# Reordering three pieces of work around the score row of a two-layer graph kernel

## The chip, the cores and the metric

The kernel runs on one core of one Trainium2 chip. The metric is the device time of one execution in microseconds (us). The traces are of single profiled executions. TensorE, VectorE, ScalarE, GpSimd and SyncE stand in profile lines as PE, DVE, ACT, POOL and SP (SPq is SyncE's own queue, from which it starts transfers).

## The reference, cut to what matters

Sixty-four graphs of 256 nodes with 512 features each pass two layers. Everything is float32.

```python
# layer 0
agg = einsum('bij,bjf->bif', adj, x) / max(sum(adj), 1e-6)
x1  = layernorm(x + relu(concat([x, agg]) @ W.T))
# layer 1
q, k = split(x1 @ Wqk); v = x1 @ Wv
agg  = adj @ (k * mask)
w    = mask * sum(q * agg, -1) / sqrt(512)
out  = layernorm(x1 + softmax(w)[:, :, None] * v)
```

## The kernel before: the parts that the change and the argument touch

The kernel works on 32 pairs of graphs in a software pipeline. One turn of the loop `j` runs layer 0 of pair `j`, layer 1 of pair `j-1`, and the softmax and last norm of pair `j-2`. Each large product is done as seven half-size products (P1 to P7), so VectorE and GpSimd prepare sums of blocks (`x1T_s`, `x1T_i`, `xT_s`, `xT_i`, `tv`, `sa`) and VectorE and ScalarE add up results. The order of instructions on each engine is chosen when the program is built; `tc.issue_after(ins)` and `tc.keep_in_program_order` constrain that choice. `late_work` is a queue of small pieces that the program text deals out between the products.

The products of a pair need the first norm's result `x1` with features on partitions (`x1T`). VectorE transposes 32 x 32 blocks within `own` (128x512 in 0.69 us, mean of 124 in before), and SyncE then places 16 squares, each by one transfer of 64 KB (2.3 us from issue to landing, median). The same SyncE queue carries the scores: a column `d` to DRAM and back as `row`, spread over all partitions, for the softmax.

```python
def place():                                  # in before
    for a in range(P // Q):
        for b in range(P // Q):
            send(to[b*Q:(b+1)*Q, :, a], sq[a*Q:(a+1)*Q, b]...)     # one square of x1T
        if a == 0 and j > 0:
            fetch_scores(j - 1)               # row <- d; d went ahead of place()
    load_x(j + 1); ...

def softmax(j):
    vector[0] = nc.vector.reduce_max(top, rk, ...).ins      # waits for the row
    ...                                       # two pairs of exponentials on ScalarE
    nc.vector.tensor_tensor(p, p, total, op=OP.mult)
```

After the softmax VectorE has the additions of `v` (last norm), and additions that free TensorE's banks: `y<-bank,y` (`after_p7`, L556 in before, L558 in the changed kernel) and `own<-bank,own` (`after_p2` of layer 0, L547). ScalarE copies other banks and also scales the norms' results.

```python
norm0(j); mask_adj(j); sumsM[j] = adj_sums(j)      # before: ahead of layer 1's products
...
run("k h h n k h h a n b q q d n c e q q n g f p p", ...)
```

## Time and profile before

| | before |
|---|---|
| median, us (2 runs) | 2135.93 (2132.95 to 2138.91) |
| span of the profiled run, us | 2142.4 |
| mean granted TensorE clock | 0.967 |
| TensorE's recurring waits, us in all | 139.2 |
| time at half clock, us in all | 95.6 |

"Recurring waits" adds the rows of TensorE's waits that occur four times or more. "Half clock" adds the stretches that the trace grants 0.50, between 110 and 2000 us; a stretch is taken to cost half its length at most. The page line is this one (busy us, share of the span, instructions):

```profile
PE 1960.3 (92%) x6596; PEld 1259.8 (59%) x6596; DVE 1618.3 (76%) x2950; ACT 1063.4 (50%) x2565; POOL 836.0 (39%) x898
```

TensorE is busy 92%, so the whole question is about the remaining 8% and the clock.

### The profile page before, as it was taken

The page shows a single profiled execution, that of the slowest core. Times are in us where ns is not written, and L with a number is a line of the kernel's source. Part 1 is how long each engine was busy: PE and PEld are TensorE (multiplying, and loading weights), DVE is VectorE, ACT ScalarE, POOL GpSimd, SP SyncE. Part 2 cuts the span into 40 slices and gives each one's busy share as a digit, 9 for nine tenths or more (in the row PEclk, how much of TensorE's full clock was granted, in tenths as well). Part 3 has the DMA queues.
Part 4 walks back from the last instruction along what each step waited for, and adds up shares of the span by engine and source line. Part 5 has one row for each costly group of instructions (what it writes and reads, how often), then busy time and mean ns, then how long its engine had stood idle before and what let it go on. Part 6 is the DMA issues. An engine that isn't in the chain of part 4 may idle for free.

```text
span 2142.4 us, 22354 instructions
## 1 busy us (share of the span) xinstructions
PE 1960.3 (92%) x6596; PEld 1259.8 (59%) x6596; DVE 1618.3 (76%) x2950; ACT 1063.4 (50%) x2565; POOL 836.0 (39%) x898
## 2 busy tenths in 40 slices
PE   8699999999999999999999999999999989999996
PEld 4465566566565565665665665655665655665663
DVE  6568777778777778777778777788778787777785
ACT  2354555455555455554455454555454555554553
POOL 2444432444433444424444423444324444334411
PEclk9899999999999999999999999999999999999998
DMA  4322333222343323333223342223332223332211
GB/s 168 74 58 82 93 104 103 66 69 85 94 104 86 83 63 90 94 104 84 70 71 88 103 104 75 65 80 92 104 104 69 69 82 93 104 94 74 64 51 45
DMA packets 389114, 182.16 MB, mean 85 GB/s; under 512 B 272128, under 2 KB 353664, under 8 KB 388992
## 3 DMA queue, kind: packets, MB, share of 16 engines
q1 hardware_dynamic: 388992, 180.72, 31.3%
q8 instruction: 53, 0.87, 0.2%
q14 instruction: 69, 0.57, 0.1%
HBM read 114.10 MB, written 34.06 MB: 69 GB/s over the span
## 4 chain that ended last, share of the span: by engine, by line
PE 47%; DVE 32%; ACT 9%; issue 5%; DMA 4%; POOL 2%; SPq 1%; DVEq 0%; ACTq 0%; POOLq 0%
PE bank L134 47%; DVE own L426 4%; DVE v L499 4%; DVE own L427 4%; DMA out<-v 3%; DVE st L404 3%; ACT own L414 2%; ACT v L414 2%; DVE y L586 2%; DVE tv L344 2%; DVE y L556 2%; DVE own L547 2%; ACT row L487 1%; POOL x1T_i L255 1%; DVE tv L343 1%
## 5 line engine op out<-in xcount | busy, mean ns | idle before, releaser
L134 PE MATMUL bank<-w,x1T_s 128*128 128x512 f32 x512 | 283.7, 663 | 0.0
L134 PE MATMUL bank<-tv,sa 128*128 128x256 f32 x768 | 197.6, 387 | 38.0 <-ACT agg L377 38.0
L134 PE MATMUL bank<-w,xT_s 128*128 128x512 f32 x512 | 231.1, 593 | 0.0
L255 POOL TENSOR_TENSOR x1T_i<-x1T 128x256 f32<-128x256 f32 x32 | 26.8, 838 | 521.1 <-DMA x1T<-turn 480.6
L134 PEld LDWEIGHTS bank<-tv,sa 128*128 128x128 f32 x768 | 143.4, 191 | 85.3 <-ACT agg L377 50.4
L297 ACT COPY bank<-bank 128x256 f32<-128x256 f32 x192 | 68.7, 358 | 214.2 <-PE bank L134 214.2
L263 POOL TENSOR_TENSOR sa<-adj 128x256 f32<-128x256 f32 x64 | 61.5, 962 | 280.1 <-DMA adj<-adj_t 147.8
L426 DVE SCALAR_TENSOR_TENSOR own<-z,rdeg,own 128x512 f32<-128x512 f32 x128 | 165.4, 1312 | 1.1 <-ACT z L395 1.1
L319 DVE TENSOR_TENSOR bank<-bank,fifth 128x256 f32<-128x256 f32 x256 | 102.7, 427 | 76.6 <-ACT fifth L310 73.6
L134 PE MATMUL bank<-t,xT_s 128*128 128x512 f32 (+1 forms) x384 | 159.0, 523 | 0.0
L134 PE MATMUL bank<-t,x1T_s 128*128 128x512 f32 (+1 forms) x384 | 158.5, 521 | 0.0
L409 ACT ACTIVATE rstd<-mv,eps 128x2 f32<-128x2 f32 x128 | 37.9, 296 | 237.1 <-DVE mv L405 234.8
L414 ACT ACTIVATE v<-v,shift,rstd 128x512 f32<-128x512 f32 x128 | 97.2, 806 | 114.5 <-DVE shift L412 114.5
L134 PEld LDWEIGHTS bank<-w,xT_s 128*128 128x128 f32 x512 | 96.6, 190 | 96.7 <-issue 80.6
L427 DVE SCALAR_TENSOR_TENSOR own<-own,x 128x512 f32<-128x512 f32 x128 | 148.2, 1195 | 0.0
L134 PE MATMUL bank<-t_i,x1T_i 128*128 128x256 f32 x384 | 118.0, 389 | 31.8 <-POOL x1T_i L255 31.8
L134 PEld LDWEIGHTS bank<-w,x1T_s 128*128 128x128 f32 x512 | 110.1, 215 | 59.5 <-issue 47.6
L134 PE MATMUL bank<-own,adj 128*128 128x256 f32 x256 | 80.2, 442 | 69.4 <-DVE y L586 69.4
L307 ACT COPY bank<-bank 128x512 f32<-128x512 f32 x192 | 111.3, 580 | 55.3 <-PE bank L134 55.3
L134 PE MATMUL bank<-t_i,xT_i 128*128 128x256 f32 x384 | 117.1, 388 | 23.0 <-POOL xT_i L255 14.4
L134 PEld LDWEIGHTS bank<-t_i,xT_i 128*128 128x128 f32 x384 | 74.0, 194 | 102.3 <-issue 70.2
L414 ACT ACTIVATE own<-own,shift,rstd 128x512 f32<-128x512 f32 x128 | 103.9, 813 | 44.7 <-DVE shift L412 44.7
(171 smaller groups left out, 4708.7 us busy)
## 6 DMA issues: line engine op xcount, KB each, us to landing
xT<-x_t SPq DMA_DIRECT2D x64, 512.0 KB, 4.9
x<-x SPq DMA_DIRECT2D x64, 512.0 KB, 4.7
out<-v SPq DMA_DIRECT2D x64, 512.0 KB, 2.8
x1T<-turn SPq DMA_DIRECT2D x496, 64.0 KB, 2.3
adj<-adj_t SPq DMA_DIRECT2D x64, 256.0 KB, 2.9
turn<-adj SPq DMA_DIRECT2D x64, 256.0 KB, 4.8
row<-d SPq DMA_DIRECT2D x31, 256.0 KB, 5.2
wqk<-wqk_t SPq DMA_DIRECT2D x4, 512.0 KB, 5.3
```

The lines of the kernel that those rows point to most:

```text
L134: i = nc.tensor.matmul(ps, a, b, start=start, stop=True, skip_group_check=True)
L255: eng.tensor_add(i[0], a21, a22)
L263: nc.gpsimd.tensor_add(s[:, 0], a21, a22)
L297: nc.scalar.copy(q[0][:, :HF], lo)
L307: nc.scalar.copy(q[1].rearrange("p (h f) -> p h f", h=2), lo[:, None, :].to_broadcast([P, 2, HF]))
L319: nc.vector.tensor_add(q[k][:, HF:], q[k][:, HF:], fifth[0])
L344: nc.vector.tensor_sub(t2, b22, t1)
L404: nc.vector.bn_stats(st, src[:, t])
L414: nc.scalar.activation(src[:, t], src[:, t], AF.Identity, bias=shift[:, t:t + 1], scale=rstd[:, t:t + 1])
L426: nc.vector.scalar_tensor_tensor(o, z[:, k, t], rdeg[:, k, t:t + 1], o, op0=OP.mult, op1=OP.add)
L427: nc.vector.scalar_tensor_tensor(o, o, 0.0, xs[j][:, k, t], op0=OP.max, op1=OP.add)
L499: nc.vector.scalar_tensor_tensor(v[k][:, t], v[k][:, t], probs[j][:, k, t:t + 1], x1[:, k, t], op0=OP.mult, op1=OP.add)
```

## The change

Its intent, as far as the diff shows: cure the three waits that lead TensorE's list in before. The first layer norm goes behind the additions of P2 onto `q` (L587), so that they free the bank in time; GpSimd's sums of the masked adjacency move one turn later, and its inner sums keep their program order; and eight of the 16 squares go ahead of the scores, so that `x1T` is complete earlier. The additions to `own` and `y` are tied behind the softmax. The order of TensorE's products after P2 changes a little too (`q q d n c e q q` becomes `q d q n c q e q`).

```diff
-            eng.tensor_add(i[0], a21, a22)            # and three more inner sums
+            for to, op, c, d in (...):
+                tc.keep_in_program_order(eng.tensor_tensor(to, c, d, op=op))
...
 def after_p2(fifth):                                  # layer 0
+    with behind(tops[0]):                             # behind the softmax's last product
         nc.vector.tensor_add(own[:, k, 0], o[k], own[:, k, 0])
 def after_p7(k):
+    with behind(tops[1]):
         nc.scalar.copy(yt[:, k, 1], u[k])
+    with behind(tops[0]):
         vector[0] = nc.vector.tensor_add(yt[:, k, 1], y[k], yt[:, k, 1]).ins
...
             run("i f k f", i=i, k=k, f=open1)
+            places[0](range(2))                       # eight squares
             send_scores(j - 2)
+            places[0]((2,))                           # four
+            fetch_scores(j - 2)
+            places[0]((3,))                           # four
...
+            sumsM[j - 1] = adj_sums(j - 1)            # a period later
-        norm0(j)
         mask_adj(j)
-        sumsM[j] = adj_sums(j)
...
-            run("k h h n k h h a n b q q d n c e q q n g f p p", ...)
+            run("k h h n k", k=k, h=h, n=n)
+            norm0(j, vector[0])                       # behind the P2 addition onto q
+            run("h h a n b q d q n c q e q n g f p p", ...)
```

More of the change, by code (lines that the diff above doesn't have):

```diff
@@ L28 @@
 from collections import deque
-from contextlib import ExitStack
+from contextlib import ExitStack, nullcontext
 import concourse.bass as bass
@@ L129, in run, with behind @@
             units[name].pop(0)()
-    vector = [None]
+    vector, places, tops = [None], [None], [None, None]
+    def behind(ins):
+        return tc.issue_after(ins) if ins else nullcontext()
     def mm(ps, a, b, start=False):
@@ L254, in inner_sums @@
             i = [X.i[:, r, ks] for r in range(4)]
-            eng.tensor_add(i[0], a21, a22)
-            eng.tensor_sub(i[1], i[0], a11)
-            eng.tensor_sub(i[2], a11, a21)
-            eng.tensor_sub(i[3], a12, i[1])
+            for to, op, c, d in ((i[0], OP.add, a21, a22), (i[1], OP.subtract, i[0], a11),
+                                 (i[2], OP.subtract, a11, a21), (i[3], OP.subtract, a12, i[1])):
+                tc.keep_in_program_order(eng.tensor_tensor(to, c, d, op=op))
     def adj_sums(j):
@@ L318, in last_two @@
                 for k in range(2):
-                    nc.vector.tensor_add(q[k][:, HF:], q[k][:, HF:], fifth[0])
+                    vector[0] = nc.vector.tensor_add(q[k][:, HF:], q[k][:, HF:], fifth[0]).ins
                 soon(0.8)
@@ L416, in layer_norm, with norm0 @@
         return [(0.8, lambda t=t: stats(t)) for t in range(n)], [(0.2, scale)]
-    def norm0(j):
+    def norm0(j, after=None):
         own, z, rdeg = owns[j], zs.pop(j), rdegs.pop(j)
@@ L425, in combine @@
             o = own[:, k, t]
-            nc.vector.scalar_tensor_tensor(o, z[:, k, t], rdeg[:, k, t:t + 1], o, op0=OP.mult, op1=OP.add)
+            with behind(after):
+                nc.vector.scalar_tensor_tensor(o, z[:, k, t], rdeg[:, k, t:t + 1], o, op0=OP.mult, op1=OP.add)
             nc.vector.scalar_tensor_tensor(o, o, 0.0, xs[j][:, k, t], op0=OP.max, op1=OP.add)
@@ L446, in turn, with place @@
             nc.vector.transpose(sq[:, :, k, :, t].rearrange("p b c q -> p c b q"), owns[j][:, k, t])
-        def place():
-            for a in range(P // Q):
+        def place(r):
+            for a in r:
                 for b in range(P // Q):
@@ L452, in place @@
                          sq[a * Q:(a + 1) * Q, b].rearrange("p k c t q -> p (k c t) q"))
-                if a == 0 and j > 0:
-                    fetch_scores(j - 1)
-            load_x(j + 1)
-            if j + 2 < NP:
-                load_rows(j + 2)
-        return [(0.7, lambda k=k, t=t: turn(k, t)) for k in range(2) for t in range(NT)] + [(0.0, place)]
+        places[0] = place
+        return [(0.7, lambda k=k, t=t: turn(k, t)) for k in range(2) for t in range(NT)]
     def scale_scores(j, to):
@@ L482, in softmax @@
         rk = row.rearrange("p a (k c) -> p k a c", k=2)
-        vector[0] = nc.vector.reduce_max(top, rk, axis=AX.XY, negate=True).ins
+        nc.vector.reduce_max(top, rk, axis=AX.XY, negate=True)
         total = small.tile([P, 2], F32, name="total")
@@ L488, in softmax @@
                                  accum_out=total[:, k:k + 1])
-            nc.scalar.activation(p[:, k], w[:, k * NT:(k + 1) * NT], AF.Exp, bias=top[:, k:k + 1])
+            tops[1] = nc.scalar.activation(p[:, k], w[:, k * NT:(k + 1) * NT], AF.Exp, bias=top[:, k:k + 1]).ins
         nc.vector.reciprocal(total, total)
-        nc.vector.tensor_tensor(p, p, total[:, :, None].to_broadcast([P, 2, NT]), op=OP.mult)
+        tops[0] = nc.vector.tensor_tensor(p, p, total[:, :, None].to_broadcast([P, 2, NT]), op=OP.mult).ins
     def finish(j):
@@ L546, in after_p2 @@
             for k in range(2):
-                nc.vector.tensor_add(own[:, k, 0], o[k], own[:, k, 0])
+                with behind(tops[0]):
+                    nc.vector.tensor_add(own[:, k, 0], o[k], own[:, k, 0])
             add_fifth(own[:, :, 0, HF:], fifth)
@@ L554, in after_p7 @@
         def after_p7(k):
-            nc.scalar.copy(yt[:, k, 1], u[k])
-            add = nc.vector.tensor_add(yt[:, k, 1], y[k], yt[:, k, 1])
-            vector[0] = add.ins
+            with behind(tops[1]):
+                nc.scalar.copy(yt[:, k, 1], u[k])
+            with behind(tops[0]):
+                vector[0] = nc.vector.tensor_add(yt[:, k, 1], y[k], yt[:, k, 1]).ins
             soon()
@@ L585, in after_p2 @@
             for k in range(2):
-                nc.vector.tensor_add(q[:, k], o[k], q[:, k])
+                vector[0] = nc.vector.tensor_add(q[:, k], o[k], q[:, k]).ins
             add_fifth(q[:, :, HF:], fifth)
@@ L652, in resnorm_kernel @@
             run("i k i k i k i k", i=i, k=k)
+            places[0](range(4))
         else:
             run("i f k f", i=i, k=k, f=open1)
+            places[0](range(2))
             send_scores(j - 2)
+            places[0]((2,))
+            fetch_scores(j - 2)
+            places[0]((3,))
             run("i f k f i f k i f k", i=i, k=k, f=open1)
-        flush()
+        if j > 0:
+            sumsM[j - 1] = adj_sums(j - 1)
+            load_x(j)
+            if j + 1 < NP:
+                load_rows(j + 1)
         run("m p p m p p", m=m, p=p)
@@ L704, in resnorm_kernel @@
             open1 = pairs(u2, Y, A22, W1["T4"], b4) + pairs(y2, Y, S4, W1["B22"], b3)
-            run("k h h n k h h a n b q q d n c e q q n g f p p", k=k, h=h, n=n, q=q, p=open1, **g)
+            run("k h h n k", k=k, h=h, n=n)
+            norm0(j, vector[0])
+            run("h h a n b q d q n c q e q n g f p p", h=h, n=n, q=q, p=open1, **g)
+            flush()
             b8()
             py, pu = pu, py
+        else:
+            norm0(0)
+            flush()
     j = NP - 1
@@ L715, in resnorm_kernel @@
     flush()
+    sumsM[j] = adj_sums(j)
     T = sums_T(owns[j])
```

## The prediction

> **What bounds the kernel now.** I read the page, then TensorE's waits, then the timeline of one steady period, then SyncE's own rows in it. The loop runs 32 times; the score maximum (L483) recurs every 64.9 us, so about 30 such periods make the span. The waits, in total, times and longest:
>
> ```profile
> PE bank L134 <- DVE y L586: 69.4, 30, 2.8
> PE bank L134 <- ACT agg L377: 38.0, 31, 2.1
> PE bank L134 <- POOL x1T_i L255: 31.8, 32, 2.9
> ```
>
> That is 2.3, 1.2 and 1.0 us per period. The first in the timeline (start, length):
>
> ```profile
> 1027.87 2.88 DVE L426 SCALAR_TENSOR_TENSOR own<-z,rdeg,own 128x512 f32<-128x512 f32 x2
> ...
> 1030.67 2.88 DVE L427 SCALAR_TENSOR_TENSOR own<-own,x 128x512 f32<-128x512 f32 x2
> ...
> 1033.48 1.28 DVE L586 TENSOR_TENSOR y<-bank,y 128x512 f32<-128x512 f32 x2
> ...
> 1034.81 1.93 PE L134 MATMUL bank<-own,adj 128*128 128x256 f32 x4 [2.80 <-DVE y L586]
> ```
>
> TensorE waits for a bank that L586 empties, and L586 queues behind four operations of the first layer norm (L426, L427). After such a wait the clock can halve; the window view of another period (PE clock is the third number from the end):
>
> ```profile
> 1103.28:1106.69 3.41, 1.53 (x7) 1.04 (x6) 3.41 (x6) 3.01 (x6) 2.92 (x5) 1.00 0.00 0
> 1106.69:1110.11 3.42, 3.42 (x5) 1.37 (x5) 2.54 (x7) 2.59 (x6) 0.00 (x0) 0.50 0.00 0
> ```
>
> A 3.41 us stretch at 0.50 costs 1.7 us; most periods have one. A period holds 64 matmul records of 512 columns and 140 of 256 (groups by form, counts over 32). Eight of each start 3.43 and 1.73 us apart from the next group at full clock, so TensorE needs 64 x 0.429 + 140 x 0.216 = 57.7 us. The other 7.2 us are waits, restarts and half clock. That is all that could be won: 30 x 7.2 = 216 us, 10%.
>
> Now the loop through the scores, which is what I think decides. SyncE, then VectorE, then TensorE:
>
> ```profile
> 1054.20 0.34 SPq L139 DMA_DIRECT2D d<-turned  x1
> 1054.65 2.61 SPq L139 DMA_DIRECT2D x1T<-turn  x4
> 1057.36 0.56 SPq L139 DMA_DIRECT2D row<-d  x1
> 1057.97 9.16 SPq L139 DMA_DIRECT2D x1T<-turn  x12
> ```
> ```profile
> 1062.60 0.69 DVE L483 TENSOR_REDUCE top<-row 128x2 f32<-128x512 f32 x1 [1.40 <-DMA row<-d]
> ...
> 1069.07 0.69 DVE L556 TENSOR_TENSOR y<-bank,y 128x512 f32<-128x512 f32 x1
> ```
> ```profile
> 1070.38 3.60 PE L134 MATMUL bank<-w,xT_s 128*128 128x512 f32 x8
> ```
>
> The score row lands 5.2 us after its issue; the maximum waits for it; L556 must empty a bank before the product at 1070.38 may write it, and did so 0.6 us earlier. So the scores are nearly critical already, and VectorE runs without a gap from 1065.4 on.
>
> [...] L426 and L427, beside GpSimd, have means of 1312 and 1195 ns, L499 (same form) a median of 746. [...] one square of x1T costs SyncE 0.65 to 0.76 us for 64 KB, against 2.3 us to land, so 16 block it for 12 us.
>
> **The change part by part.** I built the changed program, and read the order on each engine and which instruction each wait names.
>
> First layer norm behind L586 (now L587): no instruction more or less. VectorE now has L587 right after the sums of own. From the start of P2's last block to the product that needs the bank, TensorE has 3.9 us of other work; the block's two products take 0.9 of it and the two additions 1.3. The 2.3 us wait goes, and its half clock. But the eight operations of the norm now lie among the gathers of agg: beside GpSimd's sums of xT they take 1.1 to 1.4 us each, later 0.75. ScalarE has the scaling of own in front of the third copy of agg, and that scaling waits for VectorE's shift. Counted from the start of P2's third block, L587 is done at 5.3; then L429 1.4, the fifth 0.75, L430 and L429 1.2 each, statistics 0.65, an agg addition 0.65, L430 and L429 1.1 each, statistics 0.65, L430 0.75, L429 0.7, statistics 0.65 and 0.4 for aggregates and shift: the shift is done at 16.4, two scalings of 0.8 by 18.1, the copy (0.6) by 18.7. TensorE wants it at 15.9: the records between, at 0.216 and 0.429 us, take that long. New wait: 2.8 us, and 0.4 behind it for the addition that reads that copy. The old wait on this copy (1.2) is its smaller brother. Net of this part: 2.3 + 1.2 - 3.2, about 0.
>
> Inner sums in program order: the 1.0 us wait for x1T_i goes. Masked sums later: four GpSimd operations of 0.7 to 1.2 us leave the crowded stretch for one in which GpSimd idled 10 us for data; this shortens the contention, counted above.
>
> Squares first: eight squares go ahead of d, instead of none. They may start only when the last product that reads the old x1T ends, at 1052.9 (call it R); before, d left at R+1.3 and the row at R+4.5. Now: 4 x 0.68 + 4 x 0.77 = 5.8, d 0.45, four squares 3.1, so the row leaves at R+9.4 and the maximum starts at R+14.6 less, if all run at 0.68, 0.7: I take R+14.3 against R+9.7. Everything on VectorE behind the maximum is 4.6 us later, relative to TensorE.
>
> From the maximum, VectorE's new order puts the first y addition's start at +5.1 (0.69, 1.35 for ScalarE's exponentials, 0.47, own 0.6, two v additions 1.4, statistics 0.6), against +6.5 before. So the bank is free at R+20.2; TensorE wants it at R+17.5: a new wait of 2.7. Next, the second y addition starts at +6.4; own (0.6), four sums x1T_s (3.3), the fifth (0.6), one v addition (0.7) and 0.3 of small ones stand before or between the last two y additions (L565), which end at +12.3 and +13.7. TensorE needs the bank at +5.9, then 3.43 and 1.72 us of products and two pairs of 0.43, so it wants the first at +11.9 and the second 0.43 after it has got the first: 0.4 + 1.0 = 1.4. Then the v norm's second half follows the sums of y: (after L565: statistics 0.6, sums 1.8, v 0.7, sum 0.6, z 0.6, statistics 0.6, 0.9 of small ones and ScalarE's answer) its shift comes at +19.6, and ScalarE holds the second copy of z behind its scaling (0.8 + 0.6, so 21.2 where TensorE wants 19.8): 1.4, and the copy of the fifth behind one more: 1.4, and 0.5 for a bank copy. Sum of new waits here: 7.4 us.
>
> **Sum.** Removed per period 2.3 + 1.2 + 1.0 and one half-clock stretch (1.4 on average) = 5.9. Added 7.4 + 3.2 = 10.6; half clock comes back in most periods, partly hidden since TensorE then waits for VectorE anyway (0.5 counted). But some tails and small waits go with the old ones, about 1. Net 10.6 + 0.5 - 5.9 - 1.0 = +4.2 us. Followed as a chain: 14.3 to the maximum, 28.0 to P2's third block, 26.3 back to R: 68.6, which is +3.7. Times 30: +111 to +126. I take 2136 + 119 = 2255.
>
> **The rivals.** (1) The waits removed count and the scores still come in time: then 4.5 us of waits and 1.4 of half clock go, 30 x 5.9 = 177 us, about 1960. For it: VectorE is busy only 76%, and the change cures exactly the page's three waits. Against it: the 0.6 us of slack at 1070.38, and SyncE's 0.65 us per square, which no engine work hides. (2) The two cancel: if the second halves of the norms don't delay ScalarE's copies (7.4 becomes 4.1), the sum is +0.9 per period, 2160, within 2%. For it: my positions of ScalarE's work are off by a microsecond easily, and less contention could bring VectorE early. (3) GpSimd becomes late, since both sets of adjacency sums now precede x1T_i: eight operations of about 0.75 to 1.2 us, 6 to 8 us in an idle of over 15; it would not show.
>
> **Range and chances.** The loss hangs on a chain of some 70 us of which I know each duration, but which I laid out by hand; 2% up needs +1.4 us per period, and I have +4. An error of 3 us is possible, mostly on the good side. Range 2150 to 2325. Faster by over 2%: 0.11; within 2%: 0.14; slower by over 2%: 0.75.
>
> **What would show it.** In the changed profile TensorE's wait for L587 should be about nil, and the one for x1T_i too. SyncE should show eight squares, d, four squares, row, and the score maximum should start 14 us after the last read of x1T, with VectorE idle some 5 us more before it. TensorE should wait for L558 (first y addition) some 2.7 us per period, for L565 1.4, and for the agg copy L384 about 2.8; VectorE's mean for L429 and L430 should fall below 1.2 us. It is wrong if squares are issued much faster than 0.65 us, if the row comes in under 4 us, or if TensorE shows no wait for y: then rival 1 holds.

## The result, and the profile after

The changed kernel takes 2212.7 us (2212.23 to 2213.18, two runs), against 2135.93 us: a ratio of 1.036, 95% interval 1.030 to 1.042. Ratios here and below are of the runs of the same rounds, and not quite the ratio of the medians quoted. It is slower by more than 2%, inside the predicted range and 42 us below the predicted time.

The engines' line of the page after (same columns as above):

```profile
PE 1982.0 (90%) x6596; PEld 1263.8 (57%) x6596; DVE 1529.2 (69%) x2950; ACT 1075.2 (49%) x2565; POOL 815.6 (37%) x898
```

No instruction more on any of these engines, and VectorE even has 89 us less to do. Two groups account for it: the page's means for L429 and L430 (128 of each) are 969 and 828 ns, against 1312 and 1195 for the same operations before, which makes 91 us. The kernel is slower all the same, because TensorE waits. Its waits (total us, times, longest):

```profile
PE bank L137 <- DVE y L558: 108.8, 30, 4.8
PE bank L137 <- ACT agg L384: 47.6, 30, 2.5
PE bank L137 <- ACT fifth L312: 19.1, 25, 0.8
...
PE bank L137 <- DVE y L565: 2.5, 4, 0.6
```

The wait for L587 is gone from the list, and of the one for `x1T_i` 0.2 us are left. A new one, for the first `y` addition, is larger than those two together. Recurring waits went from 139.2 to 182.9 us, and half clock from 95.6 to 122.9 us. Now the chain behind it, in one period: SyncE, then VectorE, then TensorE (start, length, idle time before it and its releaser in brackets).

```profile
1080.29 5.29 SPq L142 DMA_DIRECT2D x1T<-turn  x8
1085.68 0.56 SPq L142 DMA_DIRECT2D d<-turned  x1
1086.29 2.61 SPq L142 DMA_DIRECT2D x1T<-turn  x4
1089.00 0.56 SPq L142 DMA_DIRECT2D row<-d  x1
```
```profile
1094.34 0.69 DVE L482 TENSOR_REDUCE top<-row 128x2 f32<-128x512 f32 x1 [5.84 <-DMA row<-d]
...
1097.90 0.69 DVE L547 TENSOR_TENSOR own<-bank,own 128x512 f32<-128x512 f32 x1 [0.79 <-PE bank L137]
1098.51 1.40 DVE L498 SCALAR_TENSOR_TENSOR v<-v,probs,own 128x512 f32<-128x512 f32 x2
...
1100.43 0.67 DVE L558 TENSOR_TENSOR y<-bank,y 128x512 f32<-128x512 f32 x1
```
```profile
1101.16 6.58 PE L137 MATMUL bank<-w,xT_s 128*128 128x512 f32 x8 [3.30 <-DVE y L558]
```

Eight squares hold SyncE for 5.3 us before `d` may leave; the row leaves 8.7 us after the first square. VectorE idles 5.84 us for the row, TensorE 3.30 us for VectorE. And the eight products that follow take 6.58 us, where they took 3.60 before (the line at 1070.38 in the prediction): the trace grants 0.50 from 1100.2 to 1107.0 us, and the wait lies just before. Note the bracket of L547: in this period an addition to `own` waits 0.79 us for TensorE, so here the row is not the last thing that `y` waits for. That comes back at d1.

### The profile page after: what moved, and what is told of

It is laid out like the page before. It is cut to its first block, busy times and chain, and to the rows that moved or that the text cites. A ratio compares the mean times of both kernels' runs of the same rounds, so it can differ in the third digit from the quotient of the medians.

```text
span 2210.5 us, 22456 instructions
## 1 busy us (share of the span) xinstructions
PE 1982.0 (90%) x6596; PEld 1263.8 (57%) x6596; DVE 1529.2 (69%) x2950; ACT 1075.2 (49%) x2565; POOL 815.6 (37%) x898
## 4 chain that ended last, share of the span: by engine, by line
PE 48%; DVE 31%; ACT 9%; issue 6%; DMA 3%; SPq 3%; POOL 1%; DVEq 0%; ACTq 0%; POOLq 0%
PE bank L137 47%; DVE st L406 6%; DVE v L498 3%; DVE own L430 3%; SPq L142 3%; DVE y L328 2%; ACT v L416 2%; ACT own L416 2%; DMA row<-d 2%; DVE y L587 2%; DVE own L547 2%; DVE y L565 1%; DVE y L558 1%; DVE mv L407 1%; DVE agg L369 1%
## 5 line engine op out<-in xcount | busy, mean ns | idle before, releaser
L137 PE MATMUL bank<-w,xT_s 128*128 128x512 f32 x512 | 287.6, 714 | 108.8 <-DVE y L558 108.8
L137 PE MATMUL bank<-w,x1T_s 128*128 128x512 f32 x512 | 260.3, 592 | 0.0
L137 PEld LDWEIGHTS bank<-w,xT_s 128*128 128x128 f32 x512 | 114.6, 230 | 247.8 <-DVE y L558 121.4
L248 POOL TENSOR_TENSOR xT_s<-xT 128x512 f32<-128x512 f32 x31 | 48.5, 1566 | 451.3 <-DMA xT<-x_t 428.0
L260 POOL TENSOR_TENSOR x1T_i<-x1T 128x256 f32<-128x256 f32 x64 | 48.3, 754 | 429.4 <-DMA x1T<-turn 391.7
L482 DVE TENSOR_REDUCE top<-row 128x2 f32<-128x512 f32 x31 | 21.3, 686 | 185.5 <-DMA row<-d 185.5
L260 POOL TENSOR_TENSOR x1T_i<-x1T_s 128x128 f32<-128x128 f32 x64 | 91.9, 1436 | 146.5 <-DVE x1T_s L248 146.5
L265 POOL TENSOR_TENSOR sa<-adj 128x256 f32<-128x256 f32 x64 | 49.2, 768 | 249.2 <-DMA adj<-adj_t 208.2
L416 ACT ACTIVATE own<-own,shift,rstd 128x512 f32<-128x512 f32 x128 | 97.2, 806 | 86.4 <-DVE shift L414 86.4
L137 PE MATMUL bank<-t_i,x1T_i 128*128 128x256 f32 x384 | 117.9, 389 | 19.9 <-ACT fifth L312 19.1
L299 ACT COPY bank<-bank 128x256 f32<-128x256 f32 x192 | 68.8, 358 | 132.0 <-PE bank L137 131.9
L137 PE MATMUL bank<-t,x1T 128*128 128x512 f32 x256 | 126.8, 600 | 0.0
```

Of the source, the lines that this page charges most:

```text
L137: i = nc.tensor.matmul(ps, a, b, start=start, stop=True, skip_group_check=True)
L248: eng.tensor_add(a(S1), a(A21), a(A22))
L260: tc.keep_in_program_order(eng.tensor_tensor(to, c, d, op=op))
L265: nc.gpsimd.tensor_add(s[:, 0], a21, a22)
L299: nc.scalar.copy(q[0][:, :HF], lo)
L416: nc.scalar.activation(src[:, t], src[:, t], AF.Identity, bias=shift[:, t:t + 1], scale=rstd[:, t:t + 1])
```

## The experiments

The first two rows are of the two runs that each kernel had for the result. Every other kernel ran three rounds against the kernel before, on the same chip as it, in three sessions on three chips (the kernel before had medians of 2143.1, 2137.1 and 2142.4 us there). The table has all of them; recurring waits and half clock are those of the profiled run (the 10.2 of m2 are one stretch that begins at 1999.4 us, in the program's tail).

| run | median us | ratio to before | waits, us | half clock, us |
|---|---|---|---|---|
| before (own profile) | 2135.9 | 1 | 139.2 | 95.6 |
| changed kernel | 2212.7 | 1.036 | 182.9 | 122.9 |
| u1, scores first again | 2036.5 | 0.951 | 73.9 | 0 |
| u2, norm back | 2272.8 | 1.062 | 228.9 | 139.9 |
| a1, before + norm part | 2068.6 | 0.966 | 94.3 | 27.3 |
| u4, y and own untied | 2241.6 | 1.047 | 217.7 | 184.3 |
| m1, u1 + sums back | 2071.6 | 0.971 | 94.1 | 30.7 |
| d1, four squares first | 2294.9 | 1.074 | 238.5 | 150.2 |
| n1, own behind y | 2251.9 | 1.051 | 214.1 | 109.2 |
| n3, d1 + own behind y | 2206.1 | 1.031 | 202.5 | 81.9 |
| n2, y next after softmax | 2163.2 | 1.010 | 147.5 | 78.5 |
| m3, u1 + v scaling later | 2088.5 | 0.977 | 103.7 | 64.8 |
| m2, u1 + own scaling later | 2029.2 | 0.950 | 70.9 | 10.2 |
| m4, see below | 2085.1 | 0.974 | 103.8 | 64.8 |

A check on the accounting: the span less the waits less half of the half clock is 1955 us for before (2142.4 - 139.2 - 47.8), 1960 for u1, 1966 for the changed kernel and 1973 for d1; over all runs it stays between 1930 and 1976. So of some 250 us between the fastest and the slowest span all but 46 lie in these two columns.

### u1_scores_first: the squares' place undone alone

```diff
-            places[0](range(2))
             send_scores(j - 2)
-            places[0]((2,))
+            places[0]((0,))
             fetch_scores(j - 2)
-            places[0]((3,))
+            places[0](range(1, 4))
```

> The changed kernel with only the order of the sends put back: d, one group of four squares, the row, then the other twelve. My theory (the row leaves SyncE 4.6 us later behind eight squares, so TensorE waits for the first y addition): TensorE's wait for L558 falls from 108.8 us to under 10, VectorE's wait for the row from 185.5 to about 45 or less, the row leaves about 4.5 us after the last read of x1T instead of 9, and the time is 1990 to 2050 us, below both kernels. Rival A (the norm's new place costs the time, the order of the sends is innocent): 2190 to 2215 us, with the same wait for y. Rival B (VectorE is simply too full in this stretch): 2130 to 2180, the wait goes to another line of VectorE.

Measured: 2036.5 us, ratio 0.951 (0.948 to 0.955). TensorE's waits, then SyncE, then the product that needs the bank:

```profile
PE bank L137 <- ACT agg L384: 43.7, 30, 1.5
PE bank L137 <- POOL x1T_i L260: 30.2, 30, 1.3
...
PE bank L137 <- DVE y L558: 1.5, 3, 0.9
```
```profile
1062.14 0.34 SPq L142 DMA_DIRECT2D d<-turned  x1
1062.58 3.34 SPq L142 DMA_DIRECT2D x1T<-turn  x4
1066.02 0.56 SPq L142 DMA_DIRECT2D row<-d  x1
```
```profile
1077.85 3.60 PE L137 MATMUL bank<-w,xT_s 128*128 128x512 f32 x8
```

The wait for `y` is gone, and so is half clock; both are as the theory had it. (VectorE still waits 59.0 us for the row, where 45 or less were expected.) In this period the maximum starts at 1070.96 and the product that needs the bank at 1077.85, 6.9 us later, without a wait; in the changed kernel TensorE was ready for it at 1097.86, only 3.5 us after the maximum. The squares' place costs 176 us (2212.7 less 2036.5), with what the build makes of it: in u1 both additions to `own` also stand behind the first `y` additions, and the four sums `x1T_s` behind the sums of `y` (`tv`). The rest of the change gains about 100. No wait of TensorE for `x1T` itself shows in u1, so sending its squares first had nothing to gain there.

### u2_norm_early and a1_norm_only: the norm part taken out, and alone

```diff
 # u2: the changed kernel
-            norm0(j, vector[0])       # behind the P2 addition
+        norm0(j)                      # ahead of mask_adj(j), as before
```
```diff
 # a1: the kernel before
-        norm0(j)
+            run("k h h n k", k=k, h=h, n=n)
+            norm0(j, after_q[0])      # behind the P2 addition onto q
```

> The changed kernel with the norm put back to its old place, squares still first. My theory (the norm part helps by 1.5 to 3 us per period, the sends cost more than that): slower than the changed kernel, 2240 to 2300 us, with waits for both L558 (about 3.3 us per period) and L587 (about 2). Rival A (the norm part is what made it slow): 2130 to 2180 us.

> The kernel before with the norm part alone: norm queued behind the addition of P2 onto q, sums, sends and gather order as they were. My theory: the wait for L586 (69.4 us) and most half clock go, the wait for the x1T_i (31.8) stays, the wait for the third agg copy grows from 38 to 45 to 90 us; the time is 2030 to 2110 us. Rival (the wait only moves to the agg copy, as I predicted for this part: net about 0): 2120 to 2150 us.

Measured: u2 2272.8 us (ratio 1.062), with 62.3 us of waits for L587 beside 107.4 for L558. a1 2068.6 us (0.966, 0.963 to 0.969), with no wait for the P2 addition and 63.7 us for the third copy of `agg`. Both theories held. So the norm part is good for 3.4% on the kernel before: 45 us less of waits (139.2 to 94.3), where the prediction had about none, and 68 us less of half clock (95.6 to 27.3), which the prediction counted apart. Its new wait for `agg` is 2.1 us per period (63.7 / 30), not 3.2.

### u4_free_y: the y and own additions no longer tied behind the softmax

```diff
-            with behind(tops[1]):
-                nc.scalar.copy(yt[:, k, 1], u[k])
-            with behind(tops[0]):
-                vector[0] = nc.vector.tensor_add(...)
+            nc.scalar.copy(yt[:, k, 1], u[k])
+            vector[0] = nc.vector.tensor_add(...)    # the own addition untied likewise
```

> The changed kernel with the squares still first, but the y additions and their copies no longer tied behind the softmax; in the built order they then stand ahead of the score maximum on VectorE. My theory (the late row hurts only because the y addition that frees the bank stands behind it in VectorE's queue): the wait for the y addition after P7 falls under 10 us in total although VectorE still waits some 6 us per period for the row; the time is 2010 to 2090 us. Rival (the late row delays VectorE's whole stretch, so the wait reappears at x1T_s or the agg gather): 2150 to 2215 us.

Measured: 2241.6 us, ratio 1.047. The theory's time was missed by 150 us and more, and the time lies above the rival's range too. No wait for `y` is left, but one for a bank copy on ScalarE, which neither had named. Besides the wait: ScalarE, then SyncE and VectorE:

```profile
PE bank L137 <- ACT bank L299: 168.6, 30, 5.8
```
```profile
1057.33 0.81 ACT L416 ACTIVATE v<-v,shift,rstd 128x512 f32<-128x512 f32 x1 [1.60 <-DVE shift L414]
1058.05 0.36 ACT L299 COPY bank<-bank 128x256 f32<-128x256 f32 x1
```
```profile
1035.48 0.56 SPq L142 DMA_DIRECT2D row<-d  x1
```
```profile
1048.43 0.68 DVE L482 TENSOR_REDUCE top<-row 128x2 f32<-128x512 f32 x1
```

The copy itself takes 0.36 us, but it stands in ScalarE's queue behind the exponentials and a scaling of `v`, and these wait for the late maximum. In the trace the copy runs at 1058.05, behind the scaling (0.81 us from 1057.33), though TensorE has waited for it for 5 us. But it is not the row that makes the maximum late here. The row was sent at 1035.48; with the 5.2 us from issue to landing of before and of the changed kernel (medians) it is there at about 1040.7; VectorE never waits for it, and comes to the maximum only at 1048.43, since the build set all `y` and `own` additions ahead of it. So u4 does not test the late row. It shows that a softmax pushed back in VectorE's queue holds up ScalarE's queue, and costs more than the tie that it takes away (2241.6 against 2212.7 us).

### m1_sums_early: the masked sums back, on top of u1

```diff
-            sumsM[j - 1] = adj_sums(j - 1)
         mask_adj(j)
+        sumsM[j] = adj_sums(j)
```

> The changed kernel with the scores sent first again (2036.5 us) and, besides, the masked adjacency sums of GpSimd put back where they stood before the change, right behind the masking. This values that part of the change. The prediction took it for nothing but less contention on VectorE. Theory A (it is worth little): 2030 to 2050 us, no new wait of TensorE. Theory B (it is part of what shortens the kernel: [...] x1T_i or the xT sums come late): 2055 to 2090 us, with a larger wait for the copy of agg L384 or for x1T_i L260.

Measured: 2071.6 us, ratio 0.971 (0.967 to 0.974) against 0.951 for u1. So moving the sums later is worth 0.019 of the 2137 us of before, some 41 us (from ratios of two sessions): theory B held, with the larger wait for `agg` L384 (65.9 us instead of 43.7) and 30.7 us of half clock. The means of L429 and L430 rise a little, to 1087 and 876 ns from 1026 and 859. In the trace of before the same operations (L426, L427) take 1327 and 1247 ns where they lie wholly beside GpSimd's work (123 and 108 of them), and 725 and 681 clear of it (2 and 3); in the changed kernel L430 takes 745 beside it (64).

### d1_four_first, n1_own_behind_y, n3_four_own_behind_y: fewer squares ahead, and VectorE's order

```diff
 # d1 and n3
-            places[0](range(2))
+            places[0]((0,))
             send_scores(j - 2)
-            places[0]((2,))
+            places[0]((1,))
             fetch_scores(j - 2)
-            places[0]((3,))
+            places[0]((2, 3))
 # n1 (all eight squares ahead) and n3: after_p2 of layer 0
-                with behind(tops[0]):
+                with behind(vector[0]):             # the second y addition
                     nc.vector.tensor_add(own[:, k, 0], o[k], own[:, k, 0])
```

> Half the dose: the changed kernel with four squares of x1T ahead of the score column d instead of eight (then four squares, the score row, eight squares). With no square ahead of d the time was 2036.5 us, with eight it is 2212.7. Theory (the squares ahead of the row decide, by SyncE's issue time of 0.65 to 0.7 us each): the row leaves about 2.7 us later than with none, the reduction for the maximum starts 2.7 us later; about half of the 5.9 us per period that the full dose costs, or less, since some slack comes first: 2050 to 2110 us, and TensorE's wait for the first y addition L558 is 0.3 to 1.5 us per period (10 to 45 us in all). Rival (the order itself hurts, or the number before d does not matter as long as the row comes after eight squares): about 2200 us.

Measured: 2294.9 us, ratio 1.074 (1.070 to 1.077). With half the squares ahead it is slower than with all eight; both theories missed. VectorE in one period:

```profile
1055.17 0.69 DVE L482 TENSOR_REDUCE top<-row 128x2 f32<-128x512 f32 x1 [2.91 <-DMA row<-d]
1059.06 0.17 DVE L489 RECIPROCAL total<-total 128x2 f32<-128x2 f32 x1 [3.20 <-ACT row L486]
...
1061.65 0.69 DVE L547 TENSOR_TENSOR own<-bank,own 128x512 f32<-128x512 f32 x1 [2.05 <-PE bank L137]
```

The row is indeed earlier: the maximum starts 6.4 us before TensorE is ready for the bank (at 1061.62), nearly the 6.9 of u1. But the build, which orders the engines' work anew for each program, had set an addition to `own` ahead of the `v` and `y` additions, as in the changed kernel, and that addition waits for the P2 product, which TensorE makes just before the product that wants the bank. From the end of P2 the path own, two `v`, statistics, `y` is 3.3 us, whatever the row does: the wait in front of the product was 3.30 us in both kernels. The exponentials are late as well (3.20 us): on ScalarE they stand behind copies that wait for TensorE. Kernel before and u1 have both `own` additions behind the `y` additions. So I put that order back, with eight squares (n1) and with four (n3).

> The changed kernel, squares first as it is, with one order on VectorE put back: the two additions of P2 onto own (L547) stand behind the two first y additions (L558), as in the kernel before, where the build of the changed kernel had put one of them ahead of the v and y additions. The row stays as late as it was (maximum at R+14). Theory (the order decides part of it: the own addition waits for the P2 product that TensorE makes just before the product that wants the bank, so y cannot be earlier than 3.3 us behind that product, whatever the row does): the y addition moves up by 1.4 us (0.79 of waiting and 0.61 of work in the profiled period), TensorE's wait for L558 falls from 3.6 to about 2 us per period, the time by 45 to 90 us, to 2120 to 2170. Rival (only the row's lateness counts, own costs its 0.6 us): 2190 or more. If the time falls to 2060 or less, the order is nearly all of it.

> Four squares ahead of d (2294.9 us) with the own additions behind the y additions, as in the run that does this with eight. In the four-square run the maximum starts at R+11.4, but the own addition waits 2.05 us for TensorE and y ends at R+21. With the order put back y should end at about R+18: wait of about 0.6 us per period, time 2050 to 2130. So four squares would now be better than eight with the same order. Rival (the number of squares or their place decides, not the order on VectorE): 2200 or more.

Measured: n1 2251.9 us (ratio 1.051), slower than the changed kernel; expected was a gain. The wait for `y` fell only from 108.8 to 91.4 us, since the two `v` additions now took 2.31 us in the profiled period instead of 1.40 and the row was as late as ever, and the copy of `agg` L384 rose from 47.6 to 69.1 us. n3 2206.1 us (1.031): 0.043 less than d1, so there the order was worth some 91 us of 2137, and the wait for `y` fell from 103.2 to 41.4 us; but the 2050 to 2130 expected was missed too. Waits for ScalarE's copies of `z` (L379, 51.9 us) and `agg` (66.6) stand in its place. What follows: VectorE's order counts where the row is nearly in time (d1); where it is late (changed kernel), putting the order back gained nothing.

Put side by side, these runs separate the row from the order. Let R be the end of the last product that reads the old `x1T`; medians of 25 periods:

| | maximum starts at | wait for `y` in all, us |
|---|---|---|
| u1, `own` behind `y` | R+10.3 | 1.5 |
| n3, `own` behind `y` | R+11.4 | 41.4 |
| n1, `own` behind `y` | R+14.2 | 91.4 |
| d1, one `own` ahead | R+11.4 | 103.2 |
| changed kernel, one `own` ahead | R+14.3 | 108.8 |

With `own` behind `y`, the wait grows with the lateness of the row. With one `own` addition ahead it is long in any case: in the changed kernel that addition waits for TensorE in 24 of 30 periods (19.3 us in all), in d1 in all 30. So either of the two is enough to make TensorE wait. The builds differ in later places as well, which no run takes apart.

### n2_y_next: y directly behind the softmax

```diff
-            finish(j - 2)                            # v additions of the last norm
         run("m q q q q m", m=m, q=q)
+            finish(j - 2, vector[0])                 # held behind the y additions; own as in n1
```

> The changed kernel, squares first, row as late as it was, but on VectorE the two first y additions come next after the softmax, ahead of own and of the v additions. The y addition then ends 3.4 us after the maximum's start, at R+17.5, where TensorE wants the bank at R+17.5. Theory (the lateness of the row hurts only through what stands between it and the y addition on VectorE): the wait for L558 falls under 0.6 us per period and the time to 2060 to 2130, with some of the gain lost to waits for ScalarE's copies, since the v norm is later. Rival (the row's lateness costs whatever comes next): 2180 or more.

Measured: 2163.2 us, ratio 1.010 (1.006 to 1.014): 33 us above the expected 2060 to 2130, and below the rival's 2180. TensorE's waits:

```profile
PE bank L137 <- ACT agg L384: 82.9, 30, 3.5
PE bank L137 <- ACT z L379: 42.2, 30, 1.4
...
PE bank L137 <- DVE y L559: 11.3, 15, 2.0
```

The wait for `y` is down to 0.4 us per period, as expected, with the row as late as in the changed kernel. This regains 0.026 of the time. But 127 us above u1 remain. ScalarE's copy of `z` (L379) stands directly behind a scaling of `v` in its queue, and the `v` norm hangs on the softmax: 42.2 us, which the row can explain. The copy of `agg` (L384) stands behind the scalings of `own`, of the other norm; why these are later here no run tells. So taking one consumer out of the late row's way left at least one other.

### m3_v_scale_later: which releaser is the true one

u1 still shows 30.2 us of waits for GpSimd's `x1T_i`, though the inner sums are in program order there. The program's own wait values name another producer: the product waits for ScalarE's bank copy L299. One period of u1 (TensorE, ScalarE, GpSimd):

```profile
1026.33 0.67 PE L137 MATMUL bank<-t_i,x1T_i 128*128 128x256 f32 x2 [0.90 <-POOL x1T_i L260]
```
```profile
1024.39 1.52 ACT L416 ACTIVATE v<-v,shift,rstd 128x512 f32<-128x512 f32 x2 [0.23 <-DVE shift L414]
1025.82 0.36 ACT L299 COPY bank<-bank 128x256 f32<-128x256 f32 x1
```

The copy ends at 1026.18 and a GpSimd sum at 1026.20; the profile took the later. To tell them apart, m3 holds the two scalings of the second `v` behind that copy and leaves GpSimd alone:

```diff
+    firsts[0] = nc.scalar.copy(q[0][:, :HF], lo).ins             # the copy L299
+    with behind(firsts[0] if late else None):                    # second v only
         nc.scalar.activation(src[:, t], src[:, t], AF.Identity, bias=shift, scale=rstd)
...
-            run("s s j a b s j c d s j e k j g k f", ...)
+            run("s s j", s=s, j=jj)
+            finish_held()                                        # the second v's scaling and store
+            run("a b s j c d s j e k j g k f", ...)
```

> The changed kernel with the scores sent first again, and with ScalarE's two scalings of the second v held behind the first bank copy of layer 1's P1. GpSimd's inner sums of x1T are not touched. The profile puts 30.2 us of TensorE's waits down to these sums (x1T_i L260). Theory (the profile names the wrong releaser: the wait names of the built program say that the product needs that bank copy, which stands behind the two scalings and ends at nearly the same moment as a sum of x1T_i): the wait put down to x1T_i falls below 8 us and the time by 15 to 30 us, to 2005 to 2022. Rival (the sums of GpSimd are what TensorE waits for): the wait stays at about 30 us and the time at 2030 to 2042.

Measured: the wait put down to `x1T_i` went from 30.2 to 0.2 us, so the releaser was named wrongly. In one period:

```profile
1049.21 0.59 PE L137 MATMUL bank<-t_i,x1T_i 128*128 128x256 f32 x2
```
```profile
1049.54 0.84 POOL L260 TENSOR_TENSOR x1T_i<-x1T_s 128x128 f32<-128x128 f32 x1 [6.71 <-DVE x1T_s L248]
```

The product starts before the sum that it was said to wait for. But the time went up, to 2088.5 us (0.977 against 0.951), where a gain was expected. The wait for `agg` L384 grew from 43.7 to 71.5 us and half clock from 0 to 64.8 us. SyncE shows why, first u1, then m3:

```profile
1022.02 4.30 SPq L142 DMA_DIRECT2D out<-v  x2
1029.66 0.93 SPq L142 DMA_DIRECT2D xT<-x_t  x2
```
```profile
1046.19 12.48 SPq L142 DMA_DIRECT2D out<-v  x2
1058.78 1.39 SPq L142 DMA_DIRECT2D xT<-x_t  x2
```

Both stores of `v` precede the next load of `xT` in SyncE's queue; the second store now waits for the later scaling, and the load behind it waits along. In m3 the load leaves some 5 us later than in u1, counted from the maximum (25.4 to 26.1 us behind it in three periods, against 20.0 to 21.3), so GpSimd's sums of `xT` start about 1 us after the norm's first operation, where they started 5 us before it in u1, and run beside it. The means of those operations rise to 1282 and 1066 ns, and the copy behind the norm is late.

### m2_own_scale_later, and m4_both

```diff
 # m2
+            thirds[0] = nc.scalar.copy(r22, of(u)).ins           # third copy of agg
...
+                with behind(gate and gate[0]):                   # own's scaling, rstd likewise
                     nc.scalar.activation(src[:, t], src[:, t], AF.Identity, ...)
```

> The changed kernel with the scores sent first again, and with ScalarE's scaling of own (first layer norm) held behind the third copy of agg (L384), which TensorE waits for 43.7 us in all. Theory (the copy is late because it stands behind two scalings of 0.76 us each in ScalarE's queue): the wait for L384 falls below 10 us and the time by 20 to 45 us, to 1990 to 2017. Rival (the copy would be late anyway, or the delayed scaling makes the transposes and so the squares of x1T late): a wait of the same size elsewhere, time 2030 or more.

> A try for a better kernel: scores sent first (2036.5 us), own scalings behind the third agg copy (alone: 2029.2 us, wait for L384 gone) and the two scalings of the second v behind layer 1's first bank copy (alone: 2088.5 us, the wait put down to x1T_i gone, but the wait for L384 up from 43.7 to 71.5 us). Theory (the loss of the second was the larger L384 wait, which the first takes away): 1990 to 2025 us, neither wait above 10 us. Rival (the later v scalings delay VectorE's dot products and sums all the same): 2040 or more.

Measured: m2 2029.2 us, ratio 0.950 (0.947 to 0.953). The wait for L384 is gone, but the time is that of u1 within the interval, since other waits came:

```profile
PE bank L137 <- POOL x1T_i L260: 35.7, 31, 1.5
PE bank L137 <- DVE agg L385: 20.0, 31, 1.4
```

m4 was to be m2 and m3 together. Another version ran: it named the own scalings later in the program text but did not hold them behind the copy, and the build put them back where they were, so that ScalarE's order is that of m3. It repeats m3: 2085.1 us, L384 72.2 us. Whether the two together gain is open.

## Why the prediction was right or wrong

The verdict, slower, was right, and the path that it rests on is there: the eight squares ahead hold SyncE, the row is late, and TensorE waits for a bank that VectorE empties behind the softmax. With VectorE's order of `own` and `y` held, that wait follows the row (table at n3); with the sends in their old order, 176 us go (u1). The path was not complete: the order that the build chose makes TensorE wait too (point 2). And that the time came within 42 us of the prediction is partly luck, since errors of both signs cancel (point 7). Point by point:

1. **Squares and row.** Predicted was the maximum at R+14.3; the median is R+14.3. The row leaves at R+9.0, predicted R+9.4, since eight squares took 5.29 us, not 5.8.
2. **The wait for L558.** Predicted 2.7 us per period, measured 3.6 (108.8 / 30). The missing term: the own addition, set ahead of it, was counted at its 0.6 us of work only, but waits for P2's product, 0.79 us in the period shown. From that product to the end of `y` the path takes 3.3 us, and where `own` waits, an earlier row would not have shortened the wait.
3. **The waits behind it** were mis-sized: L565 1.4, second `z` copy 1.4, fifth 1.4, bank copy 0.5, together 4.7 us. Measured are 2.5, 4.9, 19.1 and about 0 us in all, 0.9 us per period. VectorE kept to its plan (in the period shown the two L565 end 12.3 and 14.1 us after the maximum's start; predicted 12.3 and 13.7), but TensorE came later: in 26 of 30 periods half clock stretched the eight products, which the prediction gave 3.43 us, to between 5.0 and 6.6 us (from start to the next product). In the other four they took 3.54, and just there the four waits for L565 stand (0.6 us each), and the wait for the `z` copy is 0.9 us where it is at most 0.5 in the rest. So half clock hid some of these waits, not all that is missing: in the four periods they come to 2.4 us. The prediction took half clock as a cost on top, not as time in which the other engines come level.
4. **The norm part.** "About 0" for its waits was wrong; in a1 they fall by 1.5 us per period (139.2 less 94.3, over 30), and the time by 3.4%. Its old waits went as predicted (none for L587), but the new one for L384 is 1.6 us per period in the changed kernel and 2.1 in a1, not 2.8 + 0.4. A reading was wrong as well: the old wait of 1.2 us is for L377, the second copy of `agg`, and not for the third, which became L384 (L382 in before and a1, and not in the list of before). One wait went (0.7 us are left in a1) and another came. That VectorE's mean for L429 and L430 falls below 1.2 us was right: 969 and 828 ns.
5. **The wait for x1T_i** went, but not by the inner sums' order. u1 has that order and 30.2 us of the wait (a1, without it, 30.6); m3 removes it without touching GpSimd. In the changed kernel the `v` norm is so late that the copy L299 runs ahead of the second `v` scalings.
6. **Masked sums later** were left without a number; m1 puts them at some 41 us of gain.
7. **The sum.** Predicted +4.0 us per period, +119 us; measured +77 us. New waits 10.6 us predicted; the recurring waits after are 6.1 us (182.9 / 30), against 4.6 before. Half clock, predicted to fall by a net 0.9 us (1.4 less 0.5), rose by 0.45 us: half of 122.9 less 95.6, over 30. So per period the late waits were 3.8 us too high and the norm's 1.6, and against that the wait for `y` was 0.9 too low and half clock 1.35.

Of the rivals, the first (scores in time, 1960 us) describes u1, at 2036.5 us: the `agg` copy and the misnamed wait stayed. The second came near the result only by the size of the late waits, not by its verdict. GpSimd's being late, the third, never showed in TensorE's waits of the changed kernel.

Some things stay open. Why the wait for L384 is 44 us in one kernel and 83 in another is read from the trace for m3 alone; in n2, d1 and n1 the sums of `xT` also start later with respect to the norm (1.9, 2.8 and 2.7 us ahead of it, against 5.3 in u1), but no run isolates that. How much of d1's time beyond the changed kernel is the build's order on ScalarE, no run tells. And the new order of the products and the ties of `own` and `y` were never undone alone with the rest left as it was.

## What to carry to other kernels

Before you put transfers ahead of a small one that a softmax waits for, count the issue time of those transfers on the engine that starts them: here eight squares took 5.29 us of SyncE, and the maximum behind the row started at R+14.3, against R+10.3 in u1. Count a load behind a store that is not ready as well: in m3 it left some 5 us later. When one input is late, look at every queue that holds one of its consumers; freeing one can show you the next, as in n2, where the wait for `y` fell to 11.3 us and 82.9 and 42.2 us stood at ScalarE's copies. And when a program is reordered by its build, compare the built order of two versions before you take their difference for that of the line you changed.

## What the traces show of issue and clock

- One square of 64 KB costs 0.66 us of issue on SyncE in the changed kernel (5.29 us for eight), against 2.3 us to land, and eight of them put ahead of the scores cost 176 us with what the build made of it (2212.7 against 2036.5).
- In m3 two stores, the second waiting for its data, held SyncE for 12.48 us, against 4.30 in u1, and the next load left some 5 us later, counted from the maximum.
- In before a stretch of 3.41 us with 1.53 us of TensorE's work, so 1.9 us idle, was followed by half clock; in the changed kernel one with 1.07 us of work was (1096.79 to 1100.20). Between 110 and 2000 us these two traces have 54 stretches of half clock, 44 of 3.41 us and 10 of 6.83. The full clock between them, divided into stretches of 3.413 us counted back from where half clock begins, gives this: all 40 with less than 1.40 us of TensorE's work were followed by half clock, 14 of 33 with 1.40 to 1.83 us, and none of 949 with more. The length of a wait alone did not decide it: behind four of the 30 waits for L558 in the changed kernel (3.30 to 3.52 us long, where all 30 are 3.30 to 4.82) the eight products ran at full clock.
- Half clock did not simply add up with the waits behind it: in those four periods of the changed kernel these waits (point 3) were 2.4 us, in the 26 with half clock 0.1 to 1.4.
